# Local window attention in a four-layer kernel: queries evacuated by VectorE, keys and values by ScalarE, two more banks for the first projections, one division moved behind the first global scores

## The chip, the cores and the metric

The kernel runs on one core of a Trainium2 chip. Its time is device microseconds (us) for one execution; of three runs the median counts. Matrix products run on TensorE (PE in the profile, PEld for its weight loads), elementwise work on VectorE (DVE) and ScalarE (ACT), memsets and some additions on GpSimd (POOL); SP issues DMAs. A product lands in a bank of PSUM, of which a core has eight here, and another engine has to evacuate it from there before the bank can be written again.

## The reference, cut to what matters

Four layers of different kinds follow each other: a shifted-window transformer block, an edge layer, an attention with Fourier operators, and a convolution with sums over agents and time. Group normalisations stand between layers. Only the first layer is touched. For each of 4 images of 56 x 56 pixels and 128 channels, and in shortened code, it computes:

```python
# xn: the group-normalised image (32 groups)
xs   = roll(xn, (-3, -3))
wins = partition(xs)                  # 64 windows of 7 x 7 = 49 tokens
x    = reverse(mha(wins))             # 4 heads of 32 channels, within each window
xf   = x.reshape(B, 56 * 56, 128)
xf   = xf + mha(layernorm(xf))        # the same weights, over all 3136 tokens
xf   = xf + gelu(layernorm(xf) @ w1) @ w2

def mha(x):                           # wq, wk, wv, wo with biases
    q, k, v = x @ wq + bq, x @ wk + bk, x @ wv + bv       # split in 4 heads
    return softmax(q @ k.T / sqrt(32)) @ v @ wo + bo
```

## The kernel before, in words

**Frame.** `fast_layer` handles one image; it is called four times, one image after the other. It first calls `fast_windows`, which is the edited function: the attention within the windows, the layer normalisation behind it, and the first projections for the global attention. Then it computes the global attention, the second layer normalisation and the two products of the MLP. On TensorE, VectorE and ScalarE the order of instructions is the order in which the program issues them (a manual schedule); an engine whose next instruction has to wait does not go on to a later one.

**Groups.** `fast_windows` works on 8 groups of 8 windows, 392 tokens each (N = 392, NG = 8). Channels lie on the 128 partitions, tokens along the free axis. Three sets of buffers are used in turn (`w_xg` normalised input, `w_kT` keys, `w_qd` queries, `w_vd` values, `w_pT` probabilities). GpSimd sets parts of these buffers to zero or one at the start of each image (L339 to L345).

**The stages of a group** g are these functions:
- `norm` (L365): group normalisation into `w_xg`, on ScalarE for groups 0 and 1 (L368), on VectorE for the others (through `apply_norm`, L193).
- `project` (L372): takes three banks; query product (L375, one instruction), key product (L376, one), value products (L380, eight small ones). Then the evacuations. The queries of head h are the 32 partitions of that head; they are written to a block of `w_qd` of their own, so there are four of them, by `evac`, which goes to VectorE for an even second argument (L225) and to ScalarE for an odd one (L223). The keys go by one ScalarE instruction (L383), the values by two, one for each half of the partitions, by `copy` (L232 on VectorE for an even argument, L230 on ScalarE for an odd one).
- `score` (L388): eight products of keys and queries (L394) into one pair of banks (tag "ss", one buffer), and one exponential on ScalarE (L397) from there into `w_pT`. The exponential may need its function table first (ACT_TABLE_LOAD).
- `value` (L400), twice: eight products into a bank of tag "acc" (L409), reciprocal and multiplication on VectorE (L411, L412).
- `turn` (L415): four transposes (L420), two copies. `output` (L428): the output product and its evacuation to `xf`.
- `central` (L433), `variance` (L440), `root` (L447), `invert` (L451), `divide` (L454): the layer normalisation. Channels are centred by a product with a matrix; the squares of half the groups are reduced by four products into one bank; one square root on ScalarE and one VectorE reciprocal (L452) handle four groups at once: `root(0)` and `invert(0)` groups 0 to 3, `root(1)` and `invert(1)` groups 4 to 7. `divide` spreads a group's inverse deviations with a product (L459) and multiplies the centred group in place (L460, VectorE).
- `attended` (L462): global queries and keys of the group (L467, evacuated by ScalarE, L468), and the global values, four blocks of 128 tokens at a time as soon as their tokens are there (L476, evacuated by VectorE, L478).

**Order.** The loop over n (L499) issues, in one pass, stages of seven successive groups: normalisation n + 2 and projection n (in the two first passes the projection goes first), scores n - 1, values n - 2, transposes n - 3, output n - 4, centring n - 5, variance n - 6. A tail follows in written order.

**Banks.** `bank()` (L353) hands out banks for all but the local scores and values: tag "mm" with three buffers, and from `late = True` on, when no more local values are to come, "mm" and "acc" (two buffers) in turns. A request waits until the bank's last reader is done. Inside the loop the "acc" buffers are used by `value` alone, for the first time in pass n = 2.

**The image before.** From the second image on, `fast_windows` also carries the steps of `normed_images` (L1558) for the image before, the `beside` steps: statistics of the first layer's result by rows (`bn_stats`), small operations on them, the normalisation of the whole image in four pieces (L193 again, `x<-x,s_mr`), and at the end the DMAs that write it out. `run` issues one such step behind every stage once `begun` is true; the loop `for _ in steps` at the end issues what is left. The first image has no such steps.

**The end of the stage and what follows.** At the end `fast_windows` runs (attended, 1), (divide, 2), `invert(1)` and the remaining steps, and returns `rest`, a list of seven slots with the remaining projections and divisions. `fast_layer` issues one slot behind each of the first seven global scores: `scores(0)` (L827: four products of 32 rows of keys for 448 queries into the first four banks; then one exponential into `f_ring`, L830), `values(2)` (L693, two blocks of the global values), `windows_rest(n)`. The banks for the slots are three others (`other_banks`), in turns.

```python
    rest = [((attended, 2),), ((divide, 3),)] + [((attended, g), (divide, g + 1)) for g in range(3, 7)]
    rest.append(((attended, 7),))
```

## Time and profile before

| | |
|---|---|
| median of 3 runs | 3445.36 us (3444.44, 3445.36, 3445.95) |
| profiled execution | 3443.31 us, its span 3441.5 us |
| granted TensorE clock, mean | 0.997 |
| PE busy | 3317.2 us, 96% |
| PEld busy | 1425.6 us, 41% |
| DVE busy | 2651.4 us, 77% |
| ACT busy | 2134.0 us, 62% |
| POOL busy | 1284.9 us, 37% |
| first normalisation (L368) of images 1 to 4, from the span's start | 46.4, 676.0, 1309.2, 1942.6 us |

The span runs from the first to the last recorded event of the profiled execution. The busy shares are means over the whole span; the edited stage is a small part of it and occurs four times, some 633 us apart. A line of the timeline reads: start in us, duration in us, engine, line, operation, tile written<-tiles read, shapes, "x n" for n equal instructions in a row drawn together, and in brackets how long the engine had been idle and who released it. In tile names `w_` belongs to the window attention, `f_` to the global attention, `s_` to the normalisation between the layers; buffer numbers are left out.

### The profile page before, as it was taken

Reading aid. Unit: us, or ns where it says so; the run is one execution under the profiler, and the core shown is the slowest. Engines: PE = TensorE matmul, PEld = TensorE weight load, DVE = VectorE, ACT = ScalarE, POOL = GpSimd, SP = SyncE. Lnnn points to the kernel's source line nnn. Section 1 sums busy time; section 2 is a strip of 40 time slices with the busy share of each in tenths; the row PEclk is TensorE's granted clock in tenths of the full one; section 3 lists DMA queues with packets and bytes.
Section 4 is the critical chain, followed back from the end, with each engine's and each line's share of the span. In section 5 each row is a group of like instructions: output and inputs, shape, how many; then the busy total and the mean of one; then the engine's idle time right before and its main releaser. Section 6 shows DMA issues by size and latency. Waiting matters only on the chain. (4 is left out here: it accounts for less than half of the span.)

```text
span 3441.5 us, 64526 instructions
## 1 busy us (share of the span) xinstructions
PE 3317.2 (96%) x27834; PEld 1425.6 (41%) x27834; DVE 2651.4 (77%) x2552; ACT 2134.0 (62%) x2257; POOL 1284.9 (37%) x795
## 2 busy tenths in 40 slices
PE   7999999999999999999999999999999999999998
PEld 4433333353333435333343443333437443336664
DVE  6588877867888597788859858887785878895776
ACT  4688876668888575788867668887564013215442
POOL 1000007800000491000019500000685978884786
PEclk9999999999999999999999999999999999999999
DMA  2143420024344000444320034442104047743111
GB/s 107 45 93 90 97 54 20 20 51 96 88 93 89 20 1 20 102 97 97 87 48 5 20 74 93 97 91 61 38 12 110 2 96 186 189 112 94 57 20 57
DMA packets 97868, 243.42 MB, mean 71 GB/s; under 512 B 64440, under 2 KB 69816, under 8 KB 92440
## 3 DMA queue, kind: packets, MB, share of 16 engines
q0 software_dynamic: 16128, 102.77, 14.9%
q1 hardware_dynamic: 74728, 123.61, 12.3%
q10 hardware_dynamic: 6720, 12.85, 1.4%
q8 instruction: 220, 3.60, 0.4%
q14 instruction: 72, 0.59, 0.1%
HBM read 79.43 MB, written 31.33 MB: 32 GB/s over the span
## 5 line engine op out<-in xcount | busy, mean ns | idle before, releaser
L830 ACT ACTIVATE f_ring<-f_pm 128x1792 f32<-128x1792 f32 (+1 forms) x764 | 1093.8, 1482 | 226.6 <-PE f_pm L827 179.1
L682 DVE TENSOR_TENSOR f_acc<-f_acc,f_ring 128x1792 f32<-128x1792 f32 x468 | 947.7, 2025 | 191.4 <-ACT f_ring L830 161.1
L827 PE MATMUL f_pm<-f_qT,f_kT 32*128 32x448 f32 x5376 | 722.8, 571 | 9.9 <-ACT f_p L716 4.1
L672 POOL DMA_DIRECT2D f_far<-f_ring x112 | 96.5, 862 | 1327.5 <-ACT f_ring L830 1012.3
L693 PE MATMUL f_pm<-f_ring,f_va 128*32 128x448 f32 (+1 forms) x6304 | 589.4, 490 | 0.0
L1275 POOL TENSOR_TENSOR e_tp<-e_a,e_c 128x1792 f32<-128x1792 f32 (+2 forms) x172 | 480.3, 2833 | 33.4 <-issue 33.4
L1273 DVE TENSOR_TENSOR e_td<-e_a,e_pc 128x1792 f32<-128x1792 f32 (+2 forms) x292 | 478.4, 1706 | 8.8 <-ACT e_c L1261 8.8
L827 PEld LDWEIGHTS f_pm<-f_qT,f_kT 32*128 32x128 f32 x5376 | 260.1, 183 | 411.8 <-ACT f_ring L830 301.1
L693 PEld LDWEIGHTS f_pm<-f_ring,f_va 128*32 128x32 f32 x6304 | 163.9, 109 | 410.1 <-issue 397.8
L1277 ACT ACTIVATE e_tp<-e_tp 128x1792 f32<-128x1792 f32 (+2 forms) x172 | 253.3, 1495 | 98.0 <-POOL e_tp L1275 98.0
L2040 DVE TENSOR_TENSOR u_ud<-u_px,u_d 112x1792 f32<-112x1792 f32 x144 | 263.5, 1863 | 39.9 <-PE u_po L2045 35.4
L2042 POOL TENSOR_TENSOR u_up<-xh,u_d 112x1792 f32<-112x1792 f32 (+1 forms) x72 | 240.9, 3374 | 56.0 <-PE u_po L2045 39.7
L1344 PE MATMUL e_acc<-e_td,t_edge 128*32 128x448 f32 x1952 | 231.6, 542 | 6.6 <-DVE e_td L1273 6.4
L2045 PE MATMUL u_po<-u_ud,AT 112*64 112x448 f32 x1056 | 212.4, 541 | 0.5 <-DVE u_ud L2040 0.5
L1344 PE MATMUL e_acc<-e_tp,t_edge 128*32 128x448 f32 x1184 | 148.0, 543 | 23.6 <-ACT e_tp L1277 23.6
L2045 PEld LDWEIGHTS u_po<-u_ud,AT 112*64 112x64 f32 x1056 | 74.0, 137 | 126.5 <-issue 112.6
L1344 PEld LDWEIGHTS e_acc<-e_td,t_edge 128*32 128x32 f32 x1952 | 61.8, 110 | 142.4 <-issue 93.8
L737 DVE RECIPROCAL f_den<-f_den 128x448 f32<-128x448 f32 x28 | 82.6, 2951 | 44.5 <-ACT f_den L734 44.5
L1874 POOL TENSOR_TENSOR q_u<-iS,q_g 128x1792 f32<-128x1792 f32 x32 | 104.3, 3287 | 12.2 <-PE q_acc L1889 12.2
L813 POOL TENSOR_TENSOR x<-xf,xw 128x343 f32<-128x343 f32 x28 | 25.5, 909 | 222.1 <-DVE xf L802 222.1
L2145 ACT COPY x_ev<-x_po 56x896 f32<-56x896 f32 x32 | 28.8, 900 | 125.1 <-DMA x_xs<-xat 69.9
L1889 PE MATMUL q_acc<-q_u,S 64*64 64x448 f32 x1024 | 101.2, 540 | 2.1 <-DVE y L1908 1.1
(535 smaller groups left out, 4575.7 us busy)
## 6 DMA issues: line engine op xcount, KB each, us to landing
f_far<-f_ring POOLq DMA_DIRECT2D x112, 896.0 KB, 6.4
u_d<-dd SPq DMA_DIRECT2D x46, 784.0 KB
f_far<-f_ring SPq DMA_DIRECT2D x28, 896.0 KB
xw<-in_x SPq DMA_DIRECT2D x4, 1568.0 KB
x2d<-x SPq DMA_DIRECT2D x4, 1568.0 KB
xat<-x SPq DMA_DIRECT2D x4, 1568.0 KB
x_xs<-xat ACTq DMA_DIRECT2D x32, 196.0 KB
xm<-x_ev ACTq DMA_DIRECT2D x64, 98.0 KB
```

The lines of the kernel that those rows point to most:

```text
L682: nc.vector.tensor_add(e.acc, e.acc, slots(j, c))
L693: nc.tensor.matmul(e.po[heads[h], part], va[o, c, heads[h]], p, start=(c == 0), stop=(c == 23 and part.stop == NB))
L827: nc.tensor.matmul(ss[:, i, :NB], kT[heads[h], c * P:(c + 1) * P], qT[heads[h], blk(j)], start=True, stop=True)
L830: nc.scalar.activation(ring[:, slot:slot + m, :], ss[:, :m, :NB], AF.Exp, scale=scale)
L1273: nc.vector.tensor_tensor(t, am, cm, ALU.max)
L1275: nc.gpsimd.tensor_sub(t, am, cm)
L1277: nc.scalar.activation(tf, tf, AF.Relu)
L1344: nc.tensor.matmul(acc[quarters[r0 + r], :NB], w.S[:, 0, :], t[:, r].rearrange("p l n -> p (l n)"), start=(g == 0), stop=(g == len(turns) ...
L1874: nc.gpsimd.tensor_mul(u, bc(st.iS[:, bp, c, :HH], 1, HEADS), bc(g[:, n, c, :], 2, HH))
L2040: nc.vector.tensor_mul(u, bc(px[:, :, :NB], 2, m), dm)
L2042: nc.gpsimd.tensor_mul(u, bc(x, 2, m), dm)
L2045: nc.tensor.matmul(po[64 * b2:64 * b2 + 64, :NB], st.AT[:, 8 * i + h0 + q, 2 * bp + b2, :], u[:, b2, q, :], start=(left == 16), stop=(left ...
```

## The change

There are three edits in `fast_windows`.
- `bank()` takes "acc" and "mm" in turns not only when `late`, but also until `begun` is true, that is for the projections of groups 0 and 1. The six banks are acc, mm, acc for group 0 and mm, acc, mm for group 1.
- All four query evacuations of a group are issued to VectorE, both value copies to ScalarE. The keys stay on ScalarE. Before, heads 1 and 3 of the queries went to ScalarE and one of the two value copies to VectorE.
- The division of group 2 leaves the end of `fast_windows` and becomes the first slot of `rest`; the projection of group 2 shares the next slot with the division of group 3. The list still has seven slots. The line `turns += 1`, which set which bank came first at the end, goes.

```diff
-        turns = 0
+        turns, begun = 0, False
 
         def bank():
             nonlocal turns
             if source:
                 return source[0]()
-            turns += late
-            if turns % 2:
+            turns += late or not begun
+            if turns % 2 and (late or not begun):
                 return psum.tile([P, 512], F32, tag="acc", name="w_late")
             return psum.tile([P, 512], F32, tag="mm", name="w_mm", bufs=3)
...
             for h in range(4):
-                evac(k, h, qd[heads[h], h], pq[heads[h], :N].rearrange("p (w t) -> p w t", t=WIN), w.bq[heads[h]])
+                evac(k, 0, qd[heads[h], h], pq[heads[h], :N].rearrange("p (w t) -> p w t", t=WIN), w.bq[heads[h]])
             nc.scalar.activation(kT[:, :N], pk[:, :N], AF.Identity, bias=w.bk)
             for par in range(2):
-                copy(k, par, vd[halves[par], par, :, :, 0:32],
+                copy(k, 1, vd[halves[par], par, :, :, 0:32],
                      pv[halves[par]].rearrange("p (a h d) -> p a h d", a=4, h=4))
...
         norm(0)
         norm(1)
         roots[0] = psum.tile([P, 512], F32, tag="var", name="w_var", bufs=1)
-        begun = False
         for n in range(NG + 1):
             begun = n > 1
...
         root(1)
         nc.scalar.activation(eps, k.eps, AF.Exp)
-        turns += 1
-        run((attended, 1), (divide, 2))
+        run((attended, 1),)
         invert(1)
         for _ in steps:
             pass
-    rest = [((attended, 2),), ((divide, 3),)] + [((attended, g), (divide, g + 1)) for g in range(3, 7)]
+    rest = [((divide, 2),)] + [((attended, g), (divide, g + 1)) for g in range(2, 7)]
     rest.append(((attended, 7),))
```

## The prediction

> **What bounds the kernel now.** I read the table of busy stretches first, to see whether the edited stage has slack. It is the stage from the first normalisation of an image to its first global score; it runs four times.

> ```profile
> 46.40:116.40 70.00, 65.57 (x650) 42.49 (x650) 40.45 (x83) 44.79 (x77) 8.38 (x24) 1.00 0.01 1
> 676.00:749.60 73.60, 68.83 (x658) 43.38 (x657) 47.41 (x151) 48.23 (x87) 8.36 (x23) 1.00 0.06 23
> ```

> The columns are stretch, length, then busy time of PE, PE weight load, DVE, ACT and POOL, granted clock, DMA share and GB/s. The third and fourth images read like the second. The four stretches are 290.8 us of the span of 3441.5, and TensorE is busy in all but 4.4 to 4.8 us of each: it sets the pace, so what this change can win is its waits. Next I read the start of the first image in the timeline:

> ```profile
> 48.23 0.61 DVE L225 TENSOR_SCALAR w_qd<-w_mm,t_first 32x392 f32<-32x392 f32 x1 [2.60 <-PE w_mm L375]
> 48.87 0.58 ACT L223 ACTIVATE w_qd<-w_mm,t_first 32x392 f32<-32x392 f32 x1 [1.13 <-DVE w_qd L225]
> 49.49 0.62 DVE L225 TENSOR_SCALAR w_qd<-w_mm,t_first 32x392 f32<-32x392 f32 x1 [0.65 <-ACT w_qd L223]
> ...
> 50.78 0.93 PE L375 MATMUL w_mm<-w_xg,t_first 128*128 128x392 f32 x2 [0.98 <-ACT w_qd L223]
> 50.86 2.47 DVE L193 TENSOR_SCALAR w_xg<-xw,mr 128x392 f32<-128x392 f32 x1
> ...
> 55.79 0.93 PE L375 MATMUL w_mm<-w_xg,t_first 128*128 128x392 f32 x2 [1.08 <-ACT w_qd L223]
> 56.97 1.28 ACT L397 ACT_TABLE_LOAD   x1
> 58.27 0.91 ACT L397 ACTIVATE w_pT<-w_ss,t_shared 128x784 f32<-128x784 f32 x1
> ```

> Two engines share one query bank and go one after the other; the projection of the next group waits for the last of the four (0.98, then 1.08 us). ScalarE reaches its table load only at 56.97, so the second local scores (L394, start 59.24) wait 0.84 more for the exponential. That is 2.90 us; the same waits in the second image are 0.98, 0.51 and 0.84, 2.33 us. Last I read the end of the stage, in the second image:

> ```profile
> 748.05 0.69 DVE L478 COPY f_va<-w_mm 128x512 f32<-128x512 f32 x1 [2.62 <-PE w_mm L476]
> 748.90 0.56 DVE L460 TENSOR_TENSOR f_oT<-f_oT,w_late 128x392 f32<-128x392 f32 x1 [0.16 <-PE w_late L459]
> 749.38 0.50 DVE L1646 RECIPROCAL s_d<-s_d 128x56 f32<-128x56 f32 x1
> 749.61 1.03 PE L827 MATMUL f_pm<-f_qT,f_kT 32*128 32x448 f32 x8 [0.75 <-DVE f_oT L460]
> ...
> 750.08 2.60 DVE L452 RECIPROCAL f_inverse<-f_inverse 128x392 f32<-128x392 f32 x1
> 750.58 0.93 PE L467 MATMUL f_pm<-f_oT,w_fq 128*128 128x392 f32 x2
> 752.59 2.38 DVE L193 TENSOR_SCALAR x<-x,s_mr 128x784 f32<-128x784 f32 x4
> ```

> The first global scores (L827) wait 0.75 us for the division of group 2 (L460). Behind that division VectorE has 5.6 us queued, of which the row L193 x4 is work for the image before; the first image has only the reciprocal L452.

> **Part 1: banks and evacuations.** Per group VectorE gains two query evacuations (2 x 0.62) and loses one value copy (0.68): +0.56 us. ScalarE loses 2 x 0.58 and gains one copy of 0.58 (its row for the other half of the partitions; VectorE's 0.68 bounds it above): -0.58. In the first image, worked forward:
> - VectorE takes the four queries of group 0 from 48.23, each 0.62 plus a gap of 0.03, to 50.85. The normalisation of group 2 behind them starts when it does now (50.86) and ends at 53.33; the queries of group 1 then run to 55.97.
> - TensorE ends the projection of group 0 at 49.5 and starts the next at once, in a bank that is free. Its key product asks for the third "acc" buffer, of which there are two, so it waits for the queries: start 50.9 (now 51.54). Values at 51.66, local scores of group 0 at 52.58, queries of group 2 at 53.85.
> - The keys of group 2 need the bank that held the queries of group 1: 56.03, against 56.55 now. The second local scores could start 1.68 later (the spacing of 51.54 to 53.21): 57.71.
> - ScalarE has keys, values, values (to 51.05), the same for group 1 (51.8 to 54.05), table load to 55.33, exponential to 56.25: before 57.71, so that wait is gone.
> So the second local scores move from 59.24 to 57.71, -1.5; a matmul that starts from a wait takes 0.93 instead of 0.82 and one such start goes: -1.6. The second image gives the same -1.5: queries to 680.98, normalisation (1.91 us there) to 682.9, queries to 685.55, scores at 687.3 instead of 688.80. After that TensorE runs from row to row and carries the shift to the end of the stage. Bounds: 0 if VectorE is late again, -2.9 and -2.3 if all three waits went. I take -1.6 four times: it is built of rows of the same instructions.

> Where the two engines meet is the normalisation of group 2: 2.47 and 1.91 us beside POOL's memsets, 0.47 later. [...] The sum goes by the row.

> **Part 2: the division moved.** Group 2's division leaves the place before the first global scores; one slot of the remaining work is then {division 2} instead of {projection 2}, and the old slot {division 3} joins projection 2. No work is added. Call S1 to S3 the first scores.
> - S1 no longer waits for L460 but for the last key evacuation (114.88 + 0.58 in the first image): 115.52 instead of 116.36, -0.84.
> - Now: S1 116.36, projection 2 at 117.33, S2, S3, and projection 3 at 124.40: 8.04 us. After: S1, the division's product beside the exponential; S2 waits for the banks that the exponential reads: S1 + 1.23 + 1.66 + 0.05 = 2.94; S2 0.97 and values 0.89, so projection 2 at S1 + 4.80; then 2.41 (projection), 1.60 (scores 3 with a division, as in the rows 126.81 to 128.41) and 0.89: projection 3 at S1 + 9.70. That is 1.66 later from S1, 0.82 later in all. First image: -1.6 + 0.8 = -0.8.
> - In the other three images the division stands in VectorE's queue behind the reciprocal and the old image's work: L1646, L1647, L452 and L193 x4, 749.38 to 754.97 = 5.59, then L460 0.56 and hand-over 0.1. Projection 2 waits for it and all of TensorE's queue behind it: value copy end + 6.25, and projection 3 another 2.41 + 1.60 + 0.89 = 4.90 later: + 11.15. Now it is 757.66 - 748.74 = 8.92. So +2.2, and -1.6 + 2.2 = +0.6 each. Bounds: -0.84 if the later rows had room to take it up, +2.2.
> - DMA: the write of the normalised image follows L193 x4, which ends some 2 us earlier; nothing waits for it. Table loads are the same.

> **Sum.** -0.8 + 3 x 0.6 = +1.0 us. The profiled execution took 3443.31 (span 3441.5 and 1.8 around it), so 3444.3; the three timed runs have a median 2.05 above it, 3445.36: I predict 3446.4. About 0.2% (6.9 us) is what a measurement of this kernel can tell from no change.

> **Rivals.**
> - VectorE becomes the bound of the middle groups (slower). In the second to fourth images it also does the statistics of the image before: between successive local scores (693.65 to 699.42) it is busy 4.99 of 5.77 us, idle 0.78; the change adds 0.56. It decides where the 0.56 falls ahead of a transpose copy or normalisation that TensorE waits for, not into the idle 0.78 to 1.57 us. Six groups x 0.56 x three images = +10.1: 3456.5. For it: TensorE already waits 0.5 for the copies behind such a queue; against it: value copies leave that queue.
> - The delay of projection 2 is taken up, as the global scores could be paced by ScalarE. Then each image keeps -1.6 - 0.84: -9.8 and 3435.6. Against: TensorE's rows from 117.33 to 124.40 leave only 0.7 us idle.
> - The idle banks don't do what they say: with two "acc" buffers the third request waits, and only 0.4 of the shift is left: -1.6 + 7.4 = +5.8, 3451.2.

> **Chances.** Even trade 0.54, banks of little use 0.10: both within 0.2%, 0.64. VectorE bound 0.20, slower. Delay taken up 0.16, faster. The range reaches to the two outer cases, 3436 to 3456; within 0.2% alone it would be 3441 to 3452.

> **What would show it.** Right: the second local scores some 1.5 us earlier after the image's start; the wait 0.84 for the exponential gone; in three images the query product of group 2 (L467) waiting for L460 by over a us; S2 waiting for the ring's exponential. Wrong: waits of TensorE for VectorE's evacuations in groups 3 to 7, or projection 3 of the second image no later after the value copy than 8.9 us.

## The result, and the profile after

The changed kernel takes 3449.89 us (median of 20 runs, 3444.07 to 3456.18) against 3443.40 us (20 runs) before: a ratio of 1.0018, 95% interval 1.0012 to 1.0024. That is 6.5 us more, where +1.0 was predicted. The time lies inside the range and the difference within 0.2%, but it is six times the predicted step, and the interval is clear of no change at all. The profiled execution took 3446.49 us (span 3444.5), 3.2 us more than the one of before.

The table of busy stretches, from the first normalisation to the first global score, for the first and second image of the changed kernel (columns as before):

```profile
46.55:114.28 67.73, 64.81 (x644) 42.08 (x645) 44.57 (x90) 40.20 (x69) 8.39 (x24) 1.00 0.01 1
677.21:749.00 71.79, 68.08 (x656) 43.01 (x655) 52.06 (x158) 43.54 (x79) 8.36 (x23) 1.00 0.06 24
```

The stretch is shorter, as forecast: 67.73 against 70.00, 71.79 against 73.60. VectorE has taken over work from ScalarE (40.45 to 44.57). Where the shortening comes from is in TensorE's waits from 46 to 70 us; the columns are who waited, for whom, us in total, times, longest:

```profile
PE w_late L375 <- ACT w_xg L368: 1.3, 1, 1.3
PE w_mm L376 <- DVE w_qd L225: 1.0, 1, 1.0
PE w_late L376 <- DVE w_qd L225: 0.3, 1, 0.3
```

The first wait stands before too. Before, 2.1 us followed it for the query bank and 0.8 for the exponential; now 1.3 us for VectorE's queries is all.

So the loss comes later. TensorE's timeline at the first global scores of the second image (lines from L514 on are two lower than before: L825 is the old L827, L828 the old L830, L691 the old L693):

```profile
749.00 1.03 PE L825 MATMUL f_pm<-f_qT,f_kT 32*128 32x448 f32 x8 [0.96 <-ACT f_kT L468]
749.87 0.82 PE L459 MATMUL f_pm<-f_inverse,c_ones 32*128 32x392 f32 x2
751.95 1.03 PE L825 MATMUL f_pm<-f_qT,f_kT 32*128 32x448 f32 x8 [1.27 <-ACT f_ring L828]
752.92 1.43 PE L691 MATMUL f_pm<-f_ring,f_va 128*32 128x448 f32 x8
754.85 1.67 PE L467 MATMUL f_pm<-f_oT,w_fq 128*128 128x392 f32 x2 [0.49 <-DVE f_oT L460]
756.31 1.01 PE L467 MATMUL f_pm<-f_oT,w_fk 128*128 128x392 f32 x2
```

Three waits stand here within 7 us where before there was one of 0.75, and all three had been forecast (the last as over 1 us). What had not been is the second column: the values take 1.43 us instead of 0.96, the query product 1.67 instead of 0.93. The clock was lower. The trace's own record of the granted clock changes in steps of 3.413 us, and the stretches below lie on these steps (the last two 0.13 us behind them); the third column is TensorE's busy time, the third from the end the granted clock. The first three are the second image, the last two the fourth:

```profile
746.44:749.86 3.42, 2.46 (x19) 1.63 (x18) 1.78 (x2) 2.48 (x5) 0.10 (x1) 1.00 0.00 0
749.86:753.27 3.41, 2.14 (x18) 0.66 (x17) 3.38 (x6) 1.88 (x2) 0.00 (x0) 1.00 0.02 5
753.27:756.68 3.41, 2.92 (x11) 1.17 (x4) 1.52 (x3) 1.57 (x2) 0.00 (x0) 0.50 0.39 87
...
2019.75:2023.16 3.41, 2.12 (x18) 0.67 (x10) 3.38 (x5) 1.66 (x1) 0.00 (x0) 1.00 0.00 0
2023.16:2026.57 3.41, 2.47 (x17) 1.08 (x14) 1.88 (x4) 2.18 (x2) 0.00 (x0) 1.00 0.29 65
```

In the second image a window in which TensorE was busy 2.14 of 3.41 us (0.63) is followed by one at half clock. The first and third image have the same; in the fourth the window is as empty (0.62) and the clock stays. In the profile of before the emptiest window at this place is 0.78 busy, and none of the four images has a half-clock window there. Its second image:

```profile
746.25:749.66 3.41, 2.66 (x17) 1.61 (x15) 1.45 (x3) 2.65 (x5) 0.10 (x1) 1.00 0.00 0
```

The 20 runs agree: their time follows the mean clock, 3444.07 at 0.997, 3450.5 on average over the eight runs at 0.995, 3456.18 at 0.993. Their mean clock is 0.9951; 27 runs of the kernel before that list theirs have 0.9969. The difference is worth at most 0.0018 x 3445 = 6.2 us, if TensorE had work through all the slow windows. Not all of it need come from this place: keep_division and evac_only below have no half-clock window here in their profiles, and the mean clock of their runs is still only 0.9965 and 0.9962.

### The profile page after: what moved, and what is told of

It is laid out like the page before. It is cut to its first block, busy times and chain, and to the rows that moved or that the text cites. A ratio compares the mean times of both kernels' runs of the same rounds, so it can differ in the third digit from the quotient of the medians.

```text
span 3444.5 us, 64568 instructions
## 1 busy us (share of the span) xinstructions
PE 3318.8 (96%) x27834; PEld 1426.9 (41%) x27834; DVE 2671.3 (78%) x2584; ACT 2116.0 (61%) x2225; POOL 1285.0 (37%) x795
## 3 DMA queue, kind: packets, MB, share of 16 engines
q0 software_dynamic: 16128, 102.77, 14.9%
## 5 line engine op out<-in xcount | busy, mean ns | idle before, releaser
L828 ACT ACTIVATE f_ring<-f_pm 128x1792 f32<-128x1792 f32 (+1 forms) x764 | 1093.8, 1482 | 228.9 <-PE f_pm L825 182.1
L825 PE MATMUL f_pm<-f_qT,f_kT 32*128 32x448 f32 x5376 | 725.1, 571 | 15.6 <-ACT f_ring L828 5.1
L691 PE MATMUL f_pm<-f_ring,f_va 128*32 128x448 f32 (+1 forms) x6304 | 591.2, 491 | 0.0
L825 PEld LDWEIGHTS f_pm<-f_qT,f_kT 32*128 32x128 f32 x5376 | 260.0, 183 | 417.6 <-ACT f_ring L828 305.1
L691 PEld LDWEIGHTS f_pm<-f_ring,f_va 128*32 128x32 f32 x6304 | 163.8, 109 | 410.1 <-issue 397.8
L2143 ACT COPY x_ev<-x_po 56x896 f32<-56x896 f32 x32 | 28.8, 900 | 125.5 <-DMA x_xs<-xat 49.5
```

Of the source, the lines that this page charges most:

```text
L691: nc.tensor.matmul(e.po[heads[h], part], va[o, c, heads[h]], p, start=(c == 0), stop=(c == 23 and part.stop == NB))
L825: nc.tensor.matmul(ss[:, i, :NB], kT[heads[h], c * P:(c + 1) * P], qT[heads[h], blk(j)], start=True, stop=True)
L828: nc.scalar.activation(ring[:, slot:slot + m, :], ss[:, :m, :NB], AF.Exp, scale=scale)
```

## The experiments

Two measures are given for each run. The medians hold everything. The first layer's length is read image by image from the timelines: the start of the last global exponential, less the start of the first normalisation. Beside it stand the half-clock windows at the first global scores of images 1 to 4, and those after 2500 us, in the later layers, without the last ones where TensorE is out of work; the late windows were counted in the profiled executions.

| kernel | first layer against before, images 1 to 4, us | sum | half-clock windows, images 1 to 4 | late windows |
|---|---|---|---|---|
| before | 484.21, 487.90, 488.02, 489.12 in all | 0 | 0, 0, 0, 0 | 2 |
| changed | +1.11, +1.76, +1.74, +0.73 | +5.3 | 1, 1, 1, 0 | 1 |
| keep_division | -1.50, -1.22, -1.09, -1.32 | -5.1 | 0, 0, 0, 0 | 12 |
| division_only | +3.93, +2.61, +4.03, +2.63 | +13.2 | 2, 1, 2, 1 | 6 |
| filled | -0.47, +1.41, +1.54, +1.32 | +3.8 | 0, 1, 1, 1 | 5 |
| queue_behind | +2.41, -0.18, +1.51, +1.28 | +5.0 | 2, 0, 1, 1 | 12 |
| filled_whole | -0.56, +0.84, +0.96, +0.73 | +2.0 | 0, 0, 0, 0 | 6 |
| longer_wait | -0.53, +1.36, +1.53, +1.30 | +3.7 | 0, 1, 1, 1 | 2 |
| banks_only | +0.01, -0.01, -0.01, +0.02 | 0.0 | 0, 0, 0, 0 | 2 |
| evac_only | -1.52, -1.26, -1.13, -1.35 | -5.3 | 0, 0, 0, 0 | 1 |
| evac_first | -1.49, -1.21, -1.42, -1.65 | -5.8 | 0, 0, 0, 0 | 5 |
| queries_only | +0.14, +1.64, +2.01, +1.56 | +5.4 | 0, 0, 0, 0 | 2 |

**The division back at its old place (keep_division).**

```diff
 (the changed kernel)
-        run((attended, 1),)
+        turns += 1
+        run((attended, 1), (divide, 2))
...
-    rest = [((divide, 2),)] + [((attended, g), (divide, g + 1)) for g in range(2, 7)]
+    rest = [((attended, 2),), ((divide, 3),)] + [((attended, g), (divide, g + 1)) for g in range(3, 7)]
```

> The changed kernel with the division of group 2 at its old place before the first global scores (banks and evacuations as changed). Clock theory (the new waits of TensorE at the first global scores, 0.96 + 1.27 + 0.49 us within 6 us in the second image, make the chip grant a lower clock for some us behind them, and that is what costs): the waits and the drops of the clock go, the gain of the first groups stays, 4 x 1.5 = 6 us: about 3437.4 beside a before of 3443.4, and a mean clock of 0.997. Queue theory (the division stands behind 5.6 us of VectorE's work, 0.8 + 3 x 2.2 = 7.4 us, and the clock has no part): the same 6 us less, at whatever clock. Evacuation theory (VectorE's extra 0.56 us a group holds up the middle groups): little or no gain, 3442 or more, with waits of TensorE for VectorE in groups 3 to 7.

Measured: 3440.67 us against 3443.02 (ratio 0.9989, interval 0.9981 to 0.9998). The first layer is 5.1 us shorter and has no half-clock window at the first global scores. The loss of the change lies in the division's move. The median gained only 2.4 us, where 6 had been forecast, and the mean clock of the runs is 0.9965 instead of 0.997; the late windows are taken up below.

**The division's move alone (division_only).** Made to the kernel before.

```diff
-        turns += 1
-        run((attended, 1), (divide, 2))
+        run((attended, 1),)
...
-    rest = [((attended, 2),), ((divide, 3),)] + [((attended, g), (divide, g + 1)) for g in range(3, 7)]
+    rest = [((divide, 2),)] + [((attended, g), (divide, g + 1)) for g in range(2, 7)]
```

> The kernel before with nothing but the division of group 2 moved behind the first global scores. Queue theory: 0.8 + 3 x 2.2 = 7.4 us more than before, about 3450.8, the mean clock as before. Clock theory: the same waits and behind them a drop of the clock in three or four images, each about 10 us x (1 - 0.83) = 1.7 us: 7.4 + 5 to 7 = 12.5 to 14 us more, 3456 to 3457, with a mean clock of 0.995 or less. Evacuation theory: no more than 4 us slower, since most of the loss of the changed kernel would not be here.

Measured: 3454.93 us (ratio 1.0031, 1.0020 to 1.0042), 11.9 more than before, and the first layer 13.2 us longer. The queue's 7.4 us does not reach that. All four images have half-clock windows behind the first global scores, six in all. By the profile, TensorE's idle time in the four first layers is 5.7 us longer than before and its busy time, with the same products, 7.5. So the clock theory stands (its 3456 to 3457 was 1 us high): the waits alone are the smaller part.

**Idle time filled (filled, then filled_whole).** Products that nobody reads, put into TensorE's waits of the changed kernel:

```diff
         run((attended, 1),)
+        fill = psum.tile([P, 2, 512], F32, tag="ss", name="w_fill", bufs=1)
+        nc.tensor.matmul(fill[:, 0, :N], k.ones[:32, :], inverse[:32, 0, :], start=True, stop=True)
...
                 windows_rest(n)
+                if n == 0:
+                    for m in (N, N // 2):
+                        nc.tensor.matmul(pm[:, 4, :m], k.ones[:32, :], inverse[:32, 0, :m], start=True, stop=True)
```

> The changed kernel with products added that nobody reads: one spreading product (0.82 us) ahead of the first global scores, where TensorE waits 0.96 us in the second image, and one and a half (1.23 us) between the first and the second, where it waits 1.27 us. Nothing starts earlier; work is added and only idle time is filled. Queue theory and evacuation theory: the time of the changed kernel or a little more, 3450 to 3451, about 6.5 us above before. Clock theory: the drops behind the first global scores go, some 5 to 7 us of the loss with them: 3443 to 3445, and a mean clock of 0.997.

Measured: 3452.24 us (1.0029, 1.0017 to 1.0040), and three images still have the half-clock window. TensorE's timeline in the second image says why:

```profile
748.51 0.49 PE L848 MATMUL f_pm<-f_inverse,c_ones 32*128 32x392 f32 x1
748.53 0.49 PE L459 MATMUL f_pm<-f_inverse,c_ones 32*128 32x392 f32 x1
...
750.61 1.88 PE L827 MATMUL f_pm<-f_qT,f_kT 32*128 32x448 f32 x8 [0.95 <-ACT f_ring L830]
```

The added products (L848) and those of the division (L459) start 0.02 us apart and run side by side, 0.49 us each, each on 32 rows. Here they filled next to nothing: the wait of 0.95 is still there (the one ahead of the first scores is gone), and the window with it is 0.69 to 0.71 busy. So this run leaves the theory open. The next one uses products of 128 rows at the same places.

```diff
-        nc.tensor.matmul(fill[:, 0, :N], k.ones[:32, :], inverse[:32, 0, :], start=True, stop=True)
+        nc.tensor.matmul(fill[:, 0, :N], k.centre, xf[:, :N], start=True, stop=True)
...
-                        nc.tensor.matmul(pm[:, 4, :m], k.ones[:32, :], inverse[:32, 0, :m], start=True, stop=True)
+                        nc.tensor.matmul(pm[:, 4, :m], k.centre, xf[:, :m], start=True, stop=True)
```

> As the run with added products, but with products of 128 rows by 128 columns, which cannot run beside the spreading products (those of 32 rows ran two at a time, and the wait of 0.95 us ahead of the second global scores stayed): 0.82 us ahead of the first global scores and 1.23 us between the first and the second. Nobody reads them. Clock theory (a window of 3.41 us in which TensorE is busy for only 0.5 to 0.7 is followed by one at half clock, which costs up to 1.7 us): no window at these places is under 0.85 busy, no half-clock window follows, the mean clock is that of before (0.997), and though work is added the time falls to 3443 to 3446, 4 to 7 us under the changed kernel. Queue theory alone: 3450 or a little more, as the changed kernel.

Measured: 3450.37 us (1.0015, 1.0004 to 1.0027). The timeline of TensorE at the same place:

```profile
749.05 1.26 PE L848 MATMUL f_pm<-xf,c_centre 128*128 128x392 f32 x4
750.39 1.03 PE L827 MATMUL f_pm<-f_qT,f_kT 32*128 32x448 f32 x8
...
753.27 0.93 PE L467 MATMUL f_pm<-f_oT,w_fq 128*128 128x392 f32 x2 [0.96 <-DVE f_oT L460]
```

The division's products (L459) run from 748.30 to 749.12, and the added ones (L848) start at 749.05, behind them and not beside them (in filled 0.02 us apart). The wait ahead of the second global scores is gone, 0.30 us is left of the one ahead of the first, and the wait for the division (L460) stays. The window with that wait and the one behind it, within 0.1 us of the clock's steps:

```profile
750.40:753.80 3.40, 2.44 (x18) 0.84 (x19) 2.82 (x5) 1.67 (x1) 0.00 (x0) 1.00 0.01 2
753.80:757.20 3.40, 3.40 (x22) 2.02 (x20) 1.25 (x2) 1.18 (x2) 0.00 (x0) 1.00 1.12 201
```

The window is 0.72 busy, where no less than 0.85 had been expected, and still the clock stays full, in all four images. With work added, the first layer is 3.4 us shorter than in the changed kernel (+2.0 against +5.3). This is the price of the waits without the clock: -0.56, then +0.84, +0.96, +0.73, where -0.8 and three times +0.6 were predicted. But the forecast of the time, 3443 to 3446, failed: the median is the changed kernel's. The mean clock of its runs is 0.9958 and not 0.997; in the profile, which is of the slowest of its runs (3452.92), six half-clock windows lie in the later layers. So the gain at this place is shown by the first layers of one profile, not by the medians.

**The old image's work behind the division (queue_behind).** Made to the changed kernel.

```diff
         run((attended, 1),)
-        invert(1)
-        for _ in steps:
-            pass
-    rest = [((divide, 2),)] + [((attended, g), (divide, g + 1)) for g in range(2, 7)]
+    rest = [((divide, 2), (lambda g: (invert(1), list(steps)), 0))] + [((attended, g), (divide, g + 1)) for g in range(2, 7)]
```

> The changed kernel with the reciprocal of groups 4 to 7 and the rest of the old image's work issued behind the division of group 2 instead of ahead of it. Queue theory: the wait of the query product of group 2 for the division (0.49 us at the second image) and the slow start behind it go; that product starts right behind the first values, at most 1.0 us earlier in three images: some 3 us less than the changed kernel, about 3447. Clock theory: the waits of 0.96 and 1.27 us stay next to each other, so the clock still drops in most images: 3445 to 3448 with a mean clock of 0.995 to 0.996. Both alike in time; the clock of the profile behind the first global scores is what is read.

Measured: 3449.92 us (1.0021, 1.0012 to 1.0030), the changed kernel's time and not 3 us less; the clock theory's 3445 to 3448 was too low as well (mean clock 0.9943). Image 2, which has no half-clock window, shows the queue's part as expected: -0.18 against +0.73 in the changed kernel's image without one, 0.9 us gained. The other images lose it again to the clock. Two waits next to each other were enough for that (0.88 and 1.26 us in the first).

**A longer wait, without any move (longer_wait).** Made to keep_division, with one reciprocal that nobody reads:

```diff
-        run((attended, 1), (divide, 2))
+        run((attended, 1),)
+        nc.vector.reciprocal(wk.tile([P, N // 2], F32, name="w_probe"), inverse[:, 0, :N // 2])
+        run((divide, 2),)
```

> The kernel with the division at its old place (the last but for this one), with one VectorE reciprocal of 196 columns that nobody reads put between the value copy and the division of group 2: half of the row L452 of 2.60 us, 1.3 us. The first global scores wait 2.0 us in one piece instead of 0.75. Queue theory: 4 x 1.3 = 5.2 us more than without it, 3445.9 beside 3440.7, the clock as there. Clock theory: the window with that wait is 0.4 to 0.7 busy by its place on the grid, and two to four images have a half-clock window behind it: 5.2 + 3 to 7 = 8 to 12 us more, 3449 to 3453, with a mean clock of 0.995.

Measured: 3449.88 us (1.0020, 1.0011 to 1.0029), 7.2 more than the kernel before beside it, where keep_division had 2.4 less. TensorE's line at the first global scores, and the two windows on the clock's steps around it, second image:

```profile
748.95 1.03 PE L829 MATMUL f_pm<-f_qT,f_kT 32*128 32x448 f32 x8 [1.73 <-DVE f_oT L460]
```

```profile
746.50:749.90 3.40, 1.67 (x10) 0.43 (x9) 3.37 (x6) 0.79 (x2) 0.10 (x1) 1.00 0.00 0
749.90:753.30 3.40, 3.40 (x11) 2.13 (x8) 3.40 (x4) 2.51 (x3) 0.00 (x0) 0.50 0.02 5
```

The same for the first image, where the steps lie otherwise:

```profile
111.63:115.05 3.42, 2.63 (x13) 1.53 (x11) 1.60 (x2) 2.44 (x4) 0.00 (x0) 1.00 0.00 0
115.05:118.46 3.41, 2.47 (x13) 1.29 (x14) 3.30 (x3) 1.24 (x1) 0.10 (x1) 1.00 0.00 0
```

This run prices a wait. TensorE waits 1.73 instead of 0.75, 0.98 more. In the first image the wait is split over two windows (busy 0.77 and 0.72), the clock stays, and the layer is 0.97 longer than in keep_division. In the other three it falls into one (0.49 in the second image), a half-clock window follows, and the layer is 2.58 to 2.62 longer. The same wait costs 1.0 us or 2.6 us, by where it falls on the steps. One could think that in the later images the reciprocal also holds up VectorE's work for the image before, and TensorE with it. The whole first layers rule that out (length, then TensorE's busy time; first and second image of keep_division, then of this run):

```profile
45.87:528.58 482.71, 475.94 (x4077) 1.00 0.30 68
673.98:1160.65 486.67, 479.20 (x4089) 1.00 0.34 77
46.56:530.24 483.68, 475.93 (x4077) 1.00 0.30 68
675.60:1164.87 489.27, 480.86 (x4089) 1.00 0.34 77
```

TensorE's idle time is 0.98 longer in the first image and 0.94 in the second; what the second has besides is 1.66 of busy time for the same products.

**Which edit brings the gain (banks_only, evac_only).** Each made alone to the kernel before.

```diff
 (banks_only)
-            turns += late
-            if turns % 2:
+            turns += late or not begun
+            if turns % 2 and (late or not begun):
 (evac_only)
-                evac(k, h, qd[heads[h], h], ...
+                evac(k, 0, qd[heads[h], h], ...
-                copy(k, par, vd[halves[par], par, :, :, 0:32],
+                copy(k, 1, vd[halves[par], par, :, :, 0:32],
```

> The kernel before with nothing but the two idle banks for the projections of groups 0 and 1. Banks theory (the prediction's: TensorE runs ahead into free banks, and the waits of 0.98 and 0.51 to 1.08 us for the query bank go): the second local scores 1 to 1.5 us earlier, 4 to 6 us in all, 3437 to 3439. Engines theory (the pace is set by the four query evacuations, one after the other, and by ScalarE's own queue, and neither changes): second local scores unchanged, 3443, no difference that can be measured.

Measured: 3442.95 us against 3442.64 (1.0000, 0.9991 to 1.0009). The second local scores start 12.83 us after the first normalisation, before 12.82. The first ones come 0.66 earlier, and that is lost again at the second: the two banks bring nothing.

> The kernel before with nothing but the evacuations changed: all four queries on VectorE, both value copies on ScalarE. Engines theory: ScalarE is done with group 1 earlier and the exponential is no longer awaited, the second local scores come 1.3 to 1.6 us earlier, and the time is that of the kernel with the division at its old place, 3440.7 or 2 to 6 us under before. Banks theory: the query bank is still awaited, the second local scores come at most 0.8 earlier (the wait for the exponential alone), 3442 to 3443.

Measured: 3440.76 us (0.9997, 0.9987 to 1.0006); the second local scores at 11.36, the first layer 5.3 us shorter. All of the gain is the evacuations'. The median, whose interval holds no change, shows less than the first layer does.

**Only where the gain is made (evac_first).**

```diff
-                evac(k, h, qd[heads[h], h], ...
+                evac(k, 0 if g < 2 else h, qd[heads[h], h], ...
-                copy(k, par, vd[halves[par], par, :, :, 0:32],
+                copy(k, 1 if g < 2 else par, vd[halves[par], par, :, :, 0:32],
```

> The kernel before with the evacuations changed for groups 0 and 1 of each image alone; the other six groups are evacuated as before. Engines theory: the gain comes from these two groups, since it is there in full at the second local scores, and the later groups only give 0.2 us of it back in the second to fourth images (TensorE waits 0.71 us instead of 0.5 for the transpose copies of group 0): second local scores 1.4 us earlier, and 1.4 kept to the end of each image's first layer, 4 x 1.4 = 5.6 us, a little more than with all groups changed (5.3 by the profiles). In the medians some 2 to 6 us under before. If the evacuations of the later groups bring a part: less than 4 us by the profiles.

Measured: 3438.84 us against 3443.13 (0.9988, 0.9979 to 0.9997), the first layer 5.8 us shorter. Both are the lowest values here, but the interval overlaps those of evac_only and keep_division. The waits of TensorE from 676 to 700 us show a part of what the six other groups had cost. The first line is evac_only, the second this kernel:

```profile
PE w_mm L380 <- ACT w_oT L230: 0.7, 1, 0.7
```

```profile
PE w_mm L380 <- ACT w_oT L230: 0.5, 1, 0.5
```

**Half of the exchange (queries_only).** The value copies stay on both engines; made to the kernel before.

```diff
-                evac(k, h, qd[heads[h], h], ...
+                evac(k, 0, qd[heads[h], h], ...
```

> The kernel before with the four query evacuations on VectorE and the value copies left as they were (one on each engine). VectorE gets 1.24 us more a group. Engines theory: the value copy of group 0 on VectorE now stands behind its four queries and ahead of those of group 1, by 0.68 us, so the second local scores come 0.5 to 1 us later than before instead of 1.4 earlier; in the middle groups of the second to fourth images VectorE has 0.78 us of slack between two local scores and gets 1.24, so TensorE loses another 0.5 us in some of them: 0.9 us in the first image, 2 to 3 in each of the others, 7 to 10 us in all, 3450 to 3453. If moving the queries alone made the gain: 4 to 6 us under before.

Measured: 3450.42 us (1.0021, 1.0012 to 1.0030), the first layer 5.4 us longer, with no half-clock window at the first global scores. Waits of TensorE from 676 to 700 us:

```profile
PE w_ss L394 <- ACT w_pT L397: 1.1, 1, 1.1
PE w_mm L380 <- ACT w_oT L230: 0.8, 1, 0.8
```

The wait for the exponential is back, and the transpose copies are late. In the second image the local scores of groups 4 and 5 come 1.1 and 1.7 us later than before; the first image loses 0.1. The sum was forecast too high (7 to 10), and the second local scores come only 0.1 later, where 0.5 to 1 was forecast. What holds is that the queries alone bring no gain: VectorE can take them only if it gives up the values. The value copies alone were not tried.

**The late windows.** After 2500 us the profiled executions have between 1 and 12 half-clock windows, and the time from the fourth image's first normalisation to the end goes with them: 1495.8 with one (evac_only), 1498.9 with two (before), 1513.4 with twelve (keep_division). Behind the first layer the program is the same in all kernels. Why kernels without any half-clock window at the first global scores have a lower mean clock than before in some runs (evac_only 0.9962, filled_whole 0.9958) is not settled: the windows start on the clock's steps, which lie differently to the program from profile to profile (the first half-clock window starts at 32.87 us in before, at 33.06 in the changed kernel), and one profile for each kernel is too little to count them.

## Why the prediction was right, and where it was not

**Second local scores 1.5 earlier.** Measured 12.82 to 11.36 and 12.81 to 11.37: right. The reason was half wrong: the forward working let TensorE run ahead into free banks, and banks_only shows that this brings nothing. The terms that carried the result were those on VectorE's queries and on ScalarE's shorter queue, which ends the wait for the exponential; evac_only shows the two together, and queries_only that the first alone is not enough. The rival of the idle banks had it upside down: they do nothing, and the full shift remained.

**Normalisation of group 2.** The row held: 2.54 us in the first image (2.47 before), starting 0.05 us after a memset of GpSimd.

**VectorE as the bound.** Priced at 0.56 a group; it costs 0.2 to 0.3 an image, in the second to fourth. Of the shift of 1.44 in the second image 1.21 is left at the local scores of group 5, and evac_first keeps 1.43 there. The forecast left this term out of its sum and kept it as a rival.

**First global scores.** Forecast -2.4, measured 69.94 to 67.73 (-2.2) and 73.62 to 71.79 (-1.8); the wait is for the last keys, as worked out. Some 0.25 of the 0.6 missing in the second image is the term above; the rest was not taken apart.

**The division's queue.** This was the best part. From the first to the second global scores 2.94 was worked out and 2.95 measured (749.00 to 751.95). From the end of the value copy to the projection of group 2: 6.25 worked out; to that of group 3: 11.15. In the fourth image, which keeps its clock, they are 6.07 and 10.97, and the wait for the division is 0.94 where over 1 was forecast. Its lines:

```profile
2022.23 1.03 PE L825 MATMUL f_pm<-f_qT,f_kT 32*128 32x448 f32 x8 [1.29 <-ACT f_ring L828]
2023.19 0.96 PE L691 MATMUL f_pm<-f_ring,f_va 128*32 128x448 f32 x8
2025.09 0.93 PE L467 MATMUL f_pm<-f_oT,w_fq 128*128 128x392 f32 x2 [0.94 <-DVE f_oT L460]
```

The image ends +0.73, where +0.6 was forecast.

**The sum, and the step that failed.** The step that failed is the sum: it has no term for the clock. It took the durations of before's rows for TensorE behind the new waits, though the change puts three of them within 7 us. The profile of before held the warning: its clock falls to half in single windows elsewhere (at 32.87, 2586.04 and 3377.93 us). By the profiles, the first layer without half-clock windows is about -0.5 + 3 x 0.73 = +1.7 (filled_whole: +2.0) where +1.0 was predicted; three half-clock windows make it +5.3. The terms can be read one by one from the four first layers in sum (length, then TensorE's busy time) of before, keep_division and the changed kernel:

```profile
sum 1949.25, PE 1913.78; mean PE 478.45
sum 1944.11, PE 1913.87; mean PE 478.47
sum 1954.57, PE 1916.99; mean PE 479.25
```

Banks and evacuations were to bring -6.4 and bring -5.1. The division's move was to cost 7.4 of waiting, and TensorE's idle time grows by 7.3. The remaining 3.1 is more busy time for the same products, the three half-clock windows, and stood in the sum as nothing. The split into idle and busy is rough, since the profile models the ends of products: banks_only, as long as before, has 1.8 less of the one and 1.8 more of the other. What is left to the median's 6.5 lies in the later layers or in executions without a profile, and is not shown.

That the time still lies inside the range is luck. The range was drawn to two outer cases, VectorE as the bound (+10.1) and a delay that is taken up (-9.8), and neither came about.

## What to carry to other kernels

A wait of TensorE was not priced by its length alone here: the same 0.98 us more cost 0.97 in one image of longer_wait and 2.6 in three. Where a move puts several short waits next to each other on the engine that sets the pace, ask how much of any 3.413 us, the step measured here, it is still busy, and add a half-clock window (up to 1.7 us, an estimate from half of 3.413; 1.6 measured in longer_wait) where that falls towards 0.6. And change an assignment of engines only in the groups where the trace shows the wait: here two groups of eight made all of the gain, and the other six gave a part of it back (0.2 to 0.3 us at the first global scores, in three of the four images).

## What the runs showed of the hardware

```profile
3288.92:3292.33 3.41, 2.26 (x19) 1.93 (x17) 1.64 (x7) 1.58 (x3) 3.11 (x4) 1.00 0.02 5
3292.33:3326.46 34.13, 33.84 (x156) 25.27 (x158) 14.49 (x34) 12.39 (x17) 12.27 (x9) 0.50 0.00 1
```

The products that lie within the ten windows took 33.36 us, and the same ones 18.47 in the profile of before: 14.9 us more. The execution of queue_behind has ten such windows at the same products; the other profiles have none there, and division_only, filled and evac_first have three a little earlier. What starts and ends it was not tried.
- Two products of 32 rows, by the program from partitions 0 to 31 and 64 to 95, run side by side in filled (starts 748.51 and 748.53 us, 0.49 each). Added beside the division's they left the wait ahead of the second global scores at 0.95 us; products of 128 rows (filled_whole) left none there.
